# A two-layer graph kernel on one core: eight destination blocks gathered in place of nine, and 180 groups of edges counted in place of 177

## The chip, the core and the metric

The kernel runs on one core of one Trainium2 chip. Its engines are named as in the profile: PE multiplies matrices (PEld loads its stationary operand), DVE works on vectors, ACT applies functions and copies, POOL is the general engine, and SP issues DMAs. The metric is the device time of one execution in microseconds (us), as the median of several runs.

## The reference: what is computed

There are 6250 nodes with 128 features, 200000 edges with 128 features, and the edges are sorted by destination. The destinations are drawn as 6250 u² with u uniform, so low-numbered nodes receive many edges and high-numbered ones few.

```python
h = relu(layernorm(x))
x = x + relu(concat([h, segsum(h[src], dst), segsum(edge_attr, dst)]) @ W0.T + b0)
h = relu(layernorm(x))
h1 = relu(segmean(h[src], dst) @ W1_l + b1 + h @ W1_r)
h2 = relu(segmean(h1[src], dst) @ W2_l + b2 + h1 @ W2_r)
out = x + h2
```

So the sums over a node's in-edges are needed once for the edges' own features and three times (once in each of three layers) for the features of the source nodes.

## The kernel before

The nodes are cut into 49 blocks of 128 (`NB`), the edges into 196 groups of 1024 (`G`); a group holds eight tiles of 128 edges (`U`), so there are 1568 tiles.

**Two ways to sum over source nodes.** For 40 destination blocks (`NC`, the blocks 0 to 39) the kernel builds a dense matrix of counts: how many edges go from source node s to destination d. In every layer such a "dense" block then costs 49 products on PE, one for each source block, with the counts as the stationary operand and the split features (a high and a low half, 256 columns, 258 in the first layer) as the moving one: line 944. The last nine blocks (40 to 48), whose nodes have the fewest edges, are "listed" (`LISTS`): for each, a range of edge tiles is gathered by source index and summed with one product for each tile and block (line 1077).

**Stage 1, counting (up to line 816).** A set-up lays out the indices. Then a loop runs over the counted groups, 177 of them (`GC`). For each group DVE makes one-hot matrices of the sources (`sp`, line 520) and of the destinations (`sq`, line 520), weighs one of them (line 531), and, in groups where each tile has a window of its own (from group 84 on), makes a third small one-hot (`sc`). PE multiplies them tile by tile (line 755, and line 766 for the part that overlaps the tile before), and ACT copies the results into a ring buffer (line 781). The groups are cut into stretches, three groups each in the last regions; at the end of a stretch POOL writes the ring to `counts_d` in HBM (line 808). The last stretch is cut in two, the very last of one group. Between the counting products, and in proportion to the progress of the counting (`spent / shares`), PE sums the features of all 196 groups of edges (line 642; DVE makes the one-hot `hot` at line 633 and adds the result into `aggE` at line 648). The first-layer norm and product of a node block is done in every third group until all 49 are through.

**Stage 2, three layers of dense products (from line 819).** `neighbours(i)` runs over 3 x 40 dense blocks. The counts of a block come back from `counts_d` (1088 KB each, SP's queue, line 655), are widened from bytes to floats in six pieces (`widen`, line 876, some on DVE and some on ACT) and are multiplied (line 944). The rest of a block's layer, `after`, adds, norms and prepares the product of the next layer (transposition at line 460, weights at line 467); it is put between the products of the following blocks at fixed steps.

**The listed blocks** run beside the dense ones. Batches of up to three tiles (`batches`) are gathered by POOL with an indirect DMA for each tile (`gather`, line 1031), split in two halves and given a one-hot by ACT and DVE (`prepare`, lines 1048, 1049, 1055), and multiplied by PE (`sum_rows`, line 1077). The batches of a layer are spread evenly over the steps of that layer's dense products:

```python
begin = 4 * NB + NB // 2 if layer == 0 else 4 * NB
end = (NC - 2) * NB + 24 if layer < 2 else (NC - 1) * NB + 16
s = begin + (end - begin) * m // (len(batches) - 1)
```

**Which tiles a block needs, and which are counted, is fixed in constants.** The lists start at tile 1414, inside group 176, and every group up to 176 is counted, so that the two kinds of blocks meet. `GT` (176) is the group from which the indices of the listed tiles are loaded. On the chip the kernel tests that the constants fit the data (`lists_right`, line 535, and the tests from line 1131 on); where they don't, a general path computes everything again.

The constants `GC`, `GT`, `LISTS` stand at lines 36 to 40; `NC`, `NX`, `NE`, `NL` follow from them at lines 113 to 121, and the stretches at lines 123 to 138.

Of the kernel before, what the change touches and what calls it, by code (L numbers as in the profile page):

```python
# [32 lines left out]
NK = 2  # L33
NC3 = 3
PIECES = (("pair", 0, 4, 1), ("pair", 4, 8, 0), ("pair", 8, 12, 1), ("pair", 12, 17, 1), ("third", 0, 4, 0), ("third", 4, 8, 1))
GC = 177
GT = 176
LISTS = (
    (1414, 1433), (1432, 1451), (1449, 1468), (1466, 1484), (1483, 1501), (1499, 1518), (1517, 1535), (1533, 1550), (1549, 1563),
)  # L40
LATER = (1, 0, 0, 1, 0, 1)
FIRST = (1, 1, 1, 1, 0, 1)
# [45 lines left out]
def kernel(ctx: ExitStack, tc: tile.TileContext, x, srcl, dstl, edge, w0t, b0, w1l, b1, w1r, w2l, b2, w2r, out):  # L88
# [25 lines left out]
    NC = NB - NT  # L114
    NX = (G - GT) // 2
    assert 2 * NX == G - GT and U * NX <= P
    live_in_last = U - unused // P
    NE = sum(t1 - t0 for t0, t1 in LISTS)
    NL = (2 * NX - 1) * U + live_in_last
    assert LISTS[-1][1] == GT * U + NL and LISTS[0][0] >= GT * U  # L120
    CU = GC * U
    win_of = lambda g: REGIONS[min(g // RUN, NR - 1)][4]
    regions = []
    for i, reg in enumerate(REGIONS):
        if i * RUN < GC:
            regions.append((i * RUN, min((i + 1) * RUN, GC) if i + 1 < NR else GC) + reg)
    SWMAX = max(r[5] for r in regions)
# [5 lines left out]
    place_of = lambda g: sum(U // n for n in size_of[:g])  # L133
    places = place_of(GC)
    g, ng, *reg = stretches.pop()
# [4 lines left out]
    while tiles:  # L140
# [6 lines left out]
        marks = sorted((j, u) for u, (_, m) in enumerate(batch) for j in m)  # L147
        batches.append((batch[0][0] - GT * U, len(batch), marks))
    assert sum(len(marks) for _, _, marks in batches) == NE
# [56 lines left out]
    lists = build.enter_context(tc.tile_pool(name="lists", bufs=1))  # L206
    p_e = lists.tile([P, GC, U, 2], F16, name="p_e")
    q_e = lists.tile([P, GC, U, 2], F16, name="q_e")
    w_e = lists.tile([P, GC, U, 2], I16, name="w_e")
# [374 lines left out]
    def list_load(h, s):  # L584


        for k, a in enumerate((srcl, dstl)):
            at_s = bass.AP(
                tensor=a.tensor, offset=a.offset + P // U * s * GU + (GT + h * NX) * U, ap=[[U, NX], [GU, P // U], [1, U]]
            )  # L590
# [942 lines left out]
```

## Time and profile before

| | us |
|---|---|
| median of 7 runs | 1444.36 (1441.41 to 1450.07) |
| profiled execution | 1437.95 |
| its span, first to last instruction | 1436.4 |
| counting with the sums of edges | from 33.7 to about 583 |
| first layer of dense products | 584.0 to 886.5 |
| second | 886.5 to 1173.2 |
| third | 1173.2 to 1430.4 |

A row of the view by groups gives the line of the code, engine, operation, what it writes and reads, its count, its busy time and the mean of one; the idle time of the engine just before follows. The view of stretches (windows) gives each engine's busy time between two moments. PE's instructions are pipelined and overlap, so the distance between two starts says more than the duration of one. In fp32 one product is two entries on PE.

### The profile page before, as it was taken

The numbers are of one execution on the slowest core, as the hardware profiler recorded it, in microseconds if no ns is written. First come the engines' busy times: TensorE is split into PE (matmuls) and PEld (weight loads), VectorE is DVE, ScalarE is ACT, GpSimd is POOL, SyncE is SP. The second block draws the span as 40 slices with busy tenths as digits, with TensorE's granted clock in tenths as the row PEclk, the third lists the DMA queues.
The fourth block names the chain that finished last, engine by engine and source line by source line (L and its number), as shares of the span: only waits on it lengthen the run. The fifth ranks groups of instructions, "written<-read, shape, count | busy, mean of one in ns | idle before, by whom it ended". The sixth has DMA issues, their size and how long they took to land.

```text
span 1436.4 us, 37444 instructions
## 1 busy us (share of the span) xinstructions
PE 1395.3 (97%) x12457; PEld 1365.8 (95%) x12457; DVE 1152.3 (80%) x3006; ACT 933.1 (65%) x2253; POOL 693.1 (48%) x921
## 2 busy tenths in 40 slices
PE   7999999989999999899999999999999999999998
PEld 6899999889999999799999999999999999999998
DVE  8888899878898999878877787667876777777774
ACT  5434444557777777777777778666677686666663
POOL 4545676400000000366566640688887407777771
PEclk9999999999999999999999999999999999999999
DMA  2988899978999999877777766776777657777772
GB/s 77 291 269 291 283 316 323 306 268 310 329 314 311 346 348 372 294 259 246 238 245 243 245 219 213 259 258 216 231 237 235 221 193 260 267 250 261 251 253 72
DMA packets 173764, 374.02 MB, mean 260 GB/s; under 512 B 29451, under 2 KB 118985, under 8 KB 154234
## 3 DMA queue, kind: packets, MB, share of 16 engines
q1 hardware_dynamic: 121454, 268.72, 56.2%
q0 software_dynamic: 22336, 88.52, 18.1%
q10 hardware_dynamic: 29772, 14.31, 3.5%
q8 instruction: 100, 1.64, 0.5%
q14 instruction: 102, 0.84, 0.2%
HBM read 289.32 MB, written 82.13 MB: 259 GB/s over the span
## 4 chain that ended last, share of the span: by engine, by line
PE 68%; DMA 20%; issue 7%; ACT 2%; DVE 2%; POOL 0%; POOLq 0%; ACTq 0%; SPq 0%; DVEq 0%
PE ps L944 44%; DMA counts_d<-ring 17%; PE pe L642 11%; PE ps_t L1077 4%; PE pz L467 3%; PE pu L755 2%; PE pt L366 1%; DMA rows_t<-rows_d,row_i 1%; ACT wide L876 1%; DMA edge_t<-in_edge 1%; PE pu L467 1%; PE pz L460 1%; DVE wide L876 1%; PE ps L941 0%; DMA src_i<-in_src 0%
## 5 line engine op out<-in xcount | busy, mean ns | idle before, releaser
L944 PE MATMUL ps<-terms,wide 128*128 128x256 f32 (+1 forms) x5760 | 793.5, 290 | 3.4 <-DVE wide L876 1.7
L944 PEld LDWEIGHTS ps<-terms,wide 128*128 128x128 f32 x5760 | 740.0, 197 | 8.6 <-issue 1.9
L1031 POOL DMA_INDIRECT rows_t<-rows_d,row_i x447 | 505.6, 1131 | 297.4 <-issue 103.9
L642 PE MATMUL pe<-hot,edge_t 128*128 128x128 f32 x3136 | 472.9, 288 | 2.9 <-DMA edge_t<-in_edge 1.2
L642 PEld LDWEIGHTS pe<-hot,edge_t 128*128 128x128 f32 x3136 | 395.4, 192 | 6.4 <-issue 1.6
L876 ACT CAST wide<-c 128x1024 fp32r<-128x1024 uint8 x239 | 285.3, 1205 | 97.3 <-PE ps L944 87.0
L781 ACT CAST ring<-pu 128x170 f32 (+5 forms) x736 | 205.5, 282 | 86.8 <-PE pu L766 46.5
L876 DVE CAST wide<-c 128x1024 fp32r<-128x1024 uint8 x241 | 174.4, 726 | 73.6 <-PE ps L944 71.1
L755 PE MATMUL pu<-sq,sp 128*128 128x102 bf16 (+7 forms) x1416 | 170.5, 219 | 11.1 <-DVE r L470 3.8
L876 ACT CAST wide<-c_early 128x1024 fp32r<-128x1024 uint8 x118 | 140.6, 1204 | 52.4 <-PE ps L944 36.8
L808 POOL DMA_DIRECT2D counts_d<-ring x50 | 27.3, 545 | 293.7 <-ACT ring L781 213.1
L788 POOL TENSOR_TENSOR ring<-ring,fore 128x17 int32 x280 | 118.2, 422 | 82.0 <-ACT fore L776 39.2
L520 DVE TENSOR_TENSOR sq<-iota,q_e 128x816 bf16<-128x816 f16 (+7 forms) x177 | 123.5, 698 | 7.7 <-PE pu L766 7.2
L755 PEld LDWEIGHTS <-sp 128*128 128x128 bf16 x1416 | 118.9, 98 | 10.4 <-DVE sq L531 3.6
L520 DVE TENSOR_TENSOR sp<-iota,p_e 128x1024 bf16<-128x1024 f16 x177 | 121.7, 687 | 4.7 <-PE pu L755 2.2
L876 DVE CAST wide<-c_early 128x1024 fp32r<-128x1024 uint8 x122 | 88.2, 724 | 36.1 <-PE ps L944 35.1
L1055 DVE TENSOR_TENSOR tw<-rows_t,tw 128x384 fp32r<-128x384 f32 x153 | 83.2, 544 | 26.3 <-ACT tw L1048 24.8
L766 PE MATMUL pu<-sc,sp 128*128 128x17 bf16 x745 | 96.1, 172 | 0.0
L633 DVE TENSOR_TENSOR hot<-iota,rel 128x64 f32<-128x64 f16 (+13 forms) x196 | 94.5, 483 | 0.0
L790 ACT CAST ring<-pu 128x68 f32 (+5 forms) x280 | 63.3, 248 | 37.8 <-ACT fore L776 16.2
L1049 DVE TENSOR_TENSOR hot_t<-iota_p,slot_e 128x384 fp32r<-128x384 f16 (+1 forms) x153 | 87.4, 571 | 0.0
L1077 PE MATMUL ps_t<-tw,hot_t 128*128 128x256 f32 (+1 forms) x483 | 83.8, 283 | 0.0
(198 smaller groups left out, 1400.2 us busy)
## 6 DMA issues: line engine op xcount, KB each, us to landing
edge_t<-in_edge SPq DMA_DIRECT2D x196, 512.0 KB
c<-counts_d SPq DMA_DIRECT2D x80, 1088.0 KB
c_early<-counts_d SPq DMA_DIRECT2D x39, 1088.0 KB
rows_d<-feats ACTq DMA_DIRECT2D x147, 64.0 KB
r_d<-r SPq DMA_DIRECT2D x147, 64.0 KB
own<-r_d SPq DMA_DIRECT2D x147, 64.0 KB
counts_d<-ring POOLq DMA_DIRECT2D x5, 1462.0 KB
rows_t<-rows_d,row_i POOLq DMA_INDIRECT x447
```

Of the source, the lines that this page charges most:

```text
L520: made = nc.vector.tensor_tensor(to.rearrange("p t (c two) -> p t c two", two=2), iota[:, :m].rearrange("p (c two) -> p c two", two=2).uns ...
L633: nc.vector.tensor_tensor(hot[:, : U * win].rearrange("p (u w) -> p u w", w=win), iota[:, :win].unsqueeze(1).to_broadcast([P, U, win]), re ...
L642: mm = nc.tensor.matmul(ps[:, :P], e[:, u, :], hot[:, u * win : u * win + P], start=u == 0, stop=u == U - 1)
L755: mm = nc.tensor.matmul(pu[:, i * HALF : i * HALF + nq], sp[:, t, :], sq[:, t, :nq], start=t == t0, stop=t == t0 + n - 1 and n > 1,)
L766: mm = nc.tensor.matmul(pu[:, i * HALF : i * HALF + NJ], sp_b[:, t, :], sc[:, slot + 1 - len(last_tiles) + j0, :NJ], start=False, stop=j0 ...
L781: put = nc.scalar.copy(ring[:, bass.ds(to_put[(g - g0) * U + t0], nq)], pu[:, i * HALF : i * HALF + nq])
L788: add = nc.gpsimd.tensor_tensor(to, to, fore[:, i, :], op=ALU.add)
L876: copied = copy(t[:, : p1 - p0], two)
L944: dense = nc.tensor.matmul(ps[:, :m], counts, terms_of(s, s + 1)[:, 0, :m], start=s == 0, stop=s == NB - 1)
L1031: it = nc.gpsimd.indirect_dma_start(out=rows[:, u, :], out_offset=None, in_=rows_d[layer][:, :], in_offset=bass.IndirectOffsetOnAxis(ap=ro ...
L1049: made = nc.vector.tensor_tensor(hot[:, :k, :], iota_p.unsqueeze(1).to_broadcast([P, k, P]), slot_e[:, e : e + k].unsqueeze(2).to_broadcas ...
L1077: mm = nc.tensor.matmul(ps[:, :width], hot[:, k, :], tw[:, u, :width], start=begins, stop=ends)
```

## The change

`GC` goes from 177 to 180, `GT` from 176 to 178, and the first pair is taken out of `LISTS`:

```diff
-GC = 177
-GT = 176
+GC = 180
+GT = 178
 LISTS = (
-    (1414, 1433), (1432, 1451), (1449, 1468), (1466, 1484), (1483, 1501), (1499, 1518), (1517, 1535), (1533, 1550), (1549, 1563),
+    (1432, 1451), (1449, 1468), (1466, 1484), (1483, 1501), (1499, 1518), (1517, 1535), (1533, 1550), (1549, 1563),
 )
```

Block 40 becomes a dense block: `NC` is 41, and there are 123 turns of `neighbours` in place of 120. The listed tiles are 131 (1432 to 1562) in place of 149, their products 142 in place of 161 per layer, and their batches 45 in place of 51. The groups 177 to 179 are counted too; the stretches at the end are 168, 171, 174 (three groups each), 177 (two) and 179 (one), where they were 168, 171 (three each), 174 (two) and 176 (one), so one more ring is written. In the order of the source blocks, block 40 moves from the first to the last place of its piece of the widened counts.

## The prediction

> **What bounds the kernel now.** I read the busy time of each engine by stage first, then the chain of waits inside a quiet stage, then the order of time on PE and DVE in one group of the counting, and last what PE waits for. The stages (stretch, its length, then busy time and count of instructions for PE, PEld, DVE, ACT, POOL, the granted clock, DMA share, GB/s):
>
> ```profile
> 33.70:583.00 549.30, 528.47 (x5467) 510.86 (x5465) 484.04 (x1312) 327.71 (x1356) 162.01 (x353) 0.99 0.90 309
> 584.00:886.50 302.50, 297.81 (x2362) 293.33 (x2363) 237.51 (x713) 220.76 (x378) 165.04 (x152) 1.00 0.76 247
> 886.50:1173.20 286.70, 286.00 (x2272) 281.84 (x2271) 212.17 (x486) 203.82 (x329) 183.49 (x164) 1.00 0.71 232
> 1173.20:1430.40 257.20, 257.18 (x2128) 256.88 (x2126) 187.36 (x414) 161.35 (x174) 166.62 (x149) 1.00 0.71 232
> ...
> 504.30:550.50 46.20, 46.20 (x507) 45.51 (x506) 42.71 (x89) 35.80 (x119) 3.21 (x6) 1.00 0.98 354
> 550.50:577.40 26.90, 25.59 (x278) 24.73 (x277) 25.51 (x51) 18.81 (x61) 1.20 (x3) 1.00 0.92 351
> ```
>
> In the three layers (rows two to four) PE is full, at a granted clock of 1.00, while DVE has 21 to 27% and ACT 27 to 37% left. In the counting PE and DVE are both near their ends; in the last eight groups (the last row, 26.90 us, so 3.36 a group) they are equally full. "Busy" on PE can hide waits, so I take its cost from distances between starts. The chain in the third layer gives two clean ones:
>
> ```profile
> 1179.91 17.78 PE ps L944 x147
> 1197.69 0.36 PE ps_t L1077 x3
> ```
>
> 147 dense products follow each other in 17.78 us: 0.121 each. Three products of listed tiles take 0.36 with nothing lost on either side: 0.12 each.
>
> In the last region of the counting, PE in order of time:
>
> ```profile
> 564.32 0.92 PE L642 MATMUL pe<-hot,edge_t 128*128 128x128 f32 x6
> 565.07 0.24 PE L755 MATMUL pu<-sq,sp 128*128 128x187 bf16 x1
> 565.15 0.17 PE L766 MATMUL pu<-sc,sp 128*128 128x17 bf16 x1
> 565.18 0.24 PE L755 MATMUL pu<-sq,sp 128*128 128x187 bf16 x1
> 565.26 0.17 PE L766 MATMUL pu<-sc,sp 128*128 128x17 bf16 x1
> 565.28 0.69 PE L642 MATMUL pe<-hot,edge_t 128*128 128x128 f32 x4
> 565.81 0.24 PE L755 MATMUL pu<-sq,sp 128*128 128x187 bf16 x1
> ```
>
> A counted tile is a pair of products, and two pairs go from 565.07 to 565.28: 0.105 a tile. Six entries of edge sums take 0.75 (564.32 to 565.07), four take 0.53 (565.28 to 565.81): 0.11 an entry, and 0.09 more each time PE turns from counting to edges. DVE over the same group:
>
> ```profile
> 563.88 0.77 DVE L633 TENSOR_TENSOR hot<-iota,rel 128x592 f32<-128x592 f16 x1
> 564.56 0.69 DVE L520 TENSOR_TENSOR sp<-iota,p_e 128x1024 bf16<-128x1024 f16 x1
> 565.17 0.93 DVE L520 TENSOR_TENSOR sq<-iota,q_e 128x1504 bf16<-128x1504 f16 x1
> 566.02 0.23 DVE L648 TENSOR_TENSOR aggE<-aggE,pe 128x74 f32 x1
> 566.16 0.69 DVE L531 TENSOR_TENSOR sp<-sp,w_e 128x1024 bf16<-128x1024 bf16 x1
> 566.76 0.23 DVE L520 TENSOR_TENSOR sc<-iota,carry 128x144 bf16<-128x144 f16 x1
> 566.91 0.77 DVE L633 TENSOR_TENSOR hot<-iota,rel 128x592 f32<-128x592 f16 x1
> ```
>
> It never rests here. By starts, counting takes 0.61 (`sp`) + 0.85 (`sq`) + 0.60 (weighing) + 0.15 (`sc`) = 2.21, an edge group 0.68 + 0.14 = 0.82. Last, everything that PE waits for in the first layer, and POOL's gathers over the whole run:
>
> ```profile
> PE pz L460 <- ACT h L449: 2.2, 3, 1.8
> PE ps L944 <- DVE wide L876: 1.7, 4, 0.5
> PE ps L944 <- DVE aggE L648: 1.1, 1, 1.1
> PE ps L944 <- DVE terms L892: 0.5, 1, 0.5
> ...
> L1031 POOL DMA_INDIRECT rows_t<-rows_d,row_i x447 | 505.6, 1131 | 297.4 <-issue 103.9
> ```
>
> No wait of PE names a gathered row or its split (`tw`), here or in the other two layers (the second has three of 0.2, the third none).
>
> **The change, part by part.** *Block 40 dense (adds, on the path).* 49 products in each of three layers: 147 x 0.121 = 17.8 us. PE has no idle time to put them in. The block's norm, transposition and weights are done for a listed block too, and its product with `aggE` (line 941, before line 1081) as well: these only move, at nothing.
>
> *Its tiles are no longer listed (removes, on the path).* 161 - 142 = 19 products less per layer, 57 in all: 57 x 0.12 = 6.8 us back. The layers so gain 17.8 - 6.8 = 11.0.
>
> *Off the path in the layers.* Added: 18 widened pieces (nine on ACT at 1.20, nine on DVE at 0.73, the group rows' means), three `alone` copies at 0.27, and three loads of 1088 KB on SP's queue. Removed: 18 batches (ACT 0.52, DVE 0.55 + 0.55 each) and 54 gathers at 1.13 with 0.30 of issue on POOL. ACT: +10.8 - 9.4; DVE: +7.4 - 19.8; POOL: -77. The idle time of ACT and DVE (82 and 65 us in the first layer alone) hides what is added; without that cover ACT's balance would cost 1.4. The loads stand in SP's queue among those of own rows and x, four blocks ahead; at the third layer's 232 GB/s one takes 4.8 us, 14.4 in all if nothing covered them, but the DMA share is 0.71 and the gathers dropped are 54 x 64 KB, as many bytes. The batches sit at other steps of the layer (39 apart instead of 33), so the transpositions of listed blocks meet other products; of waits on ACT there are now 2.8 us in layers one and two, and I take their change as nothing, bounded by 3 either way.
>
> *Three more counted groups.* The sums of edges stay at 196 groups; they are only spread over 180. PE gets 24 tiles x 0.105 = 2.5 and about 12 more turns x 0.09 = 1.1: 3.6. DVE gets 3 x 2.21 = 6.6. ACT gets 24 copies of 0.32 (7.7), with 30% free. If PE sets the pace throughout, the stage grows by 3.6; if DVE does, by 6.6. If the new groups run at today's 3.36 and the thinner edge work gives the other 177 nothing, by 10.1. If the work falls into PE's idle time (20.3 us, the sum of PE's rows in the view of waits from 33.7 to 583, mostly for the first layer's `hT` and `r` and for one early `sq`), by nearly 0. A gain is excluded: PE, DVE and ACT all get more work here and none gets less. PE is full in the earlier regions and level with DVE in the last, so I take the middle of 3.6 and 6.6: **5.1**, with 0 and 10.1 as ends.
>
> *One more ring write.* 1598 KB on POOL's queue, 4.6 us at 354 GB/s. POOL mostly waits for ACT there (46 us of ACT against 16 of an earlier write from 504 to 583), so the write lies beside counting. The last two stretches keep their sizes (two groups and one), and what queues behind the last writes on POOL, the first gathers, is needed blocks later; the first block's counts are loaded 14 groups before the end, as now. Nothing.
>
> *Set-up.* The index tables are 180 columns wide, not 177: 12 copies on ACT at 0.8 and 192 products at 0.08 grow by 1.7%: 0.4, on the path. One index column less per load of lists: nothing.
>
> **Sum.** 11.0 + 5.1 + 0.4 = 16.5 on the profiled execution's 1437.95, so 1454.5. That execution lies 6.4 below the median of the runs shown; on 1444.36 the same sum gives **1460.9 us**, 1.1% slower.
>
> Two rules of the Trainium skill were weighed. In "TensorE: Matmul & The Clock Gate", Back-to-back issue gap, an isolated product of N columns takes N/2.4 + 2.5 ns, 109 ns for 256; the row has 121. As an estimate by that page the 147 and the 57 would be 16.0 - 6.2 = 9.8, and the whole 1459.7; the row decides. "DMA: Bandwidth & Descriptors", Rules for kernel authors, says that transfers under 64 KB mostly pay overhead and should be coalesced, which speaks for dropping 54 gathers of just that size; it would give POOL's 77 us to the kernel if they were on the path, and the waits of PE show that they are not.
>
> **The rivals.**
> - *The counting pays in full, or its end slips* (15%): the new groups run at 3.36 and nothing comes back, 10.1 + 11.0 + 0.4 = 21.5, 1465.9. For it: DMA share 0.98 at 504 to 550 and DVE without rest in the last groups, where all new work goes. Against: PE, not DVE, is full in the earlier regions, and 196 edge groups over 180 instead of 177 take 1.7% of its edge work out of each.
> - *The counting is almost free* (8%): 11.0 + 0.4, and the 2.8 us of waits for ACT go as well: 1453 to 1456. For it: 20.3 us of waits. Against: those end on the first layer's chain and stay.
> - *The other side: the gathers pace the layers* (4%). POOL works 167 us and issues 37 of the third layer's 257, after 46 us of waiting for rows: its queue is full. If a late row held PE, 18 gathers less a layer at 1.43 would bring 25.7 a layer, 77 in all, and the time 1384; it decides from 16.5 of 77 on. Against: a gather that is late shows as PE waiting at line 1077, and that wait is absent.
> - *The change doesn't do what it says* (1%): a test on the chip fails and everything is computed again. With the reference's destinations, tile 1432 begins at node 5243 (it must be 5184 to 5247) and tile 1440 at 5301 (at least 5248), and a whole last three-group stretch reaches 166 nodes of 177. The general path would take many times the kernel's time.
>
> **How the numbers follow.** The forecast has 72%. A kernel this size tells 0.3%, 4.3 us, from no change. All cases but the last two are slower by more; with waits I can't see, 92% slower, 3% within, 5% faster. The range goes from the nearly free counting, 1454.5, to the full price with 1.6 for the scatter of medians, 1467.5.
>
> **What would show it.** Line 944 at 6027 products and 0.121 from start to start; line 1077 at 426; the layers some 3.7 us longer each (306, 290.5, 261), the counting ending near 588 to 589. Wrong would be: the counting 10 or more longer; a PE wait at line 1077 that is gone; a new wait of line 944 on a load or on `wide`; or the first block's start later than the last edge sum by more than now (1.1).

## The result and the profile after

| | before | after |
|---|---|---|
| median, us | 1442.52 (46 runs, 1435.66 to 1450.07) | 1457.23 (18 runs, 1453.59 to 1462.48) |
| ratio after / before | | 1.0102, 95% interval 1.0089 to 1.0115 |
| profiled execution, us | 1437.95 | 1461.09 |

The change makes the kernel 14.7 us slower; forecast were 16.5, and 1460.9 for the time. The two profiled executions lie on opposite sides of their medians (4.6 below, 3.9 above), so they differ by 23.1, and 8.4 of that is scatter.

The profile after by stages: the stretch, its length, then busy time and count of instructions for PE, PEld, DVE, ACT, POOL, the granted clock, DMA share and GB/s. The first row is the counting, the others are the three layers.

```profile
35.00:596.00 561.00, 535.20 (x5518) 514.41 (x5515) 488.96 (x1321) 336.53 (x1380) 161.30 (x354) 0.99 0.89 306
597.17:903.30 306.13, 302.83 (x2391) 298.55 (x2392) 232.57 (x703) 221.34 (x375) 146.18 (x134) 0.99 0.75 244
903.30:1192.90 289.60, 289.22 (x2303) 285.46 (x2302) 210.24 (x479) 204.04 (x327) 156.13 (x146) 1.00 0.70 229
1192.90:1453.63 260.73, 260.73 (x2158) 260.36 (x2156) 182.92 (x406) 161.15 (x171) 148.57 (x131) 1.00 0.70 229
```

The layers grew from 302.5, 286.8 and 257.2 to 306.1, 289.6 and 260.7: by 3.6, 2.8 and 3.5, 9.9 in all. PE is full in them as before. In the chain of the third layer a product still has the same price. (Each product of line 944 is one entry: 6027 of them for 41 blocks of 49 in three layers. Two entries a product holds for the sums of edges, line 642, with 3136 entries for 1568 tiles.) 147 dense products and three listed ones read:

```profile
1199.65 17.75 PE ps L944 x147
1217.40 0.36 PE ps_t L1077 x3
```

All that PE waits for in the first layer after is 4.9 us, no item of which is a gathered row; in the second layer it is one wait of 0.3, in the third none:

```profile
PE ps L944 <- DVE wide L876: 2.1, 3, 1.1
PE ps L944 <- DVE aggE L648: 1.7, 1, 1.7
PE ps L944 <- DVE terms L892: 0.6, 1, 0.6
PE ps L944 <- ACT end_ring L781: 0.5, 1, 0.5
```

POOL's gathers fell by the 54 that were dropped, and POOL's waits grew in their place (the last part of the row):

```profile
L1031 POOL DMA_INDIRECT rows_t<-rows_d,row_i x393 | 441.0, 1122 | 367.0 <-DVE tw L1055 103.7
```

The first dense product stands at 597.2 in place of 584.0, and what PE waits for just ahead of it, the last sum of edges, grew from 1.09 to 1.73; first the kernel before, then the changed one:

```profile
584.01 0.37 PE L944 MATMUL ps<-terms,wide 128*128 128x258 f32 x1 [1.09 <-DVE aggE L648]
```

```profile
597.17 0.36 PE L944 MATMUL ps<-terms,wide 128*128 128x258 f32 x1 [1.73 <-DVE aggE L648]
```

Of the difference of the medians, 14.7, the layers take 9.9, and 4.8 is left for the counting and the set-up, if all of the scatter lies there.

**Where the counting's time went.** DVE starts one `sp` (line 520) for each group, so these starts are a clock of the counting. I read them from DVE's work in order of time; the last two columns are the kernels of the experiments e11 and e10 below, which differ only in `GC`, 177 and 180. Times in us.

| from the start of `sp` of group | before | after | e11 (177) | e10 (180) |
|---|---|---|---|---|
| 0 to 84 | 229.5 | 233.5 | 231.0 | 231.2 |
| 84 to 96 | 46.3 | 42.2 | 47.9 | 42.1 |
| 96 to 168 | 241.0 | 240.8 | 241.0 | 240.3 |
| 168 to 176 | 26.9 | 27.6 | 26.8 | 28.8 |
| 176 to 179, the three more | none | 10.6 | none | 9.8 |
| from the last `sp` to the first dense product | 6.6 | 7.5 | 7.2 | 9.1 |

So the three groups cost at least their full pace, about 3.5 each (9.8 to 14.0 over the six profiles with 180 groups whose work is whole). In groups 96 to 168 the thinner edge work gives nothing back that shows: 240.1 to 242.2 in these six, 240.8 to 242.6 in the four with 177 groups and nine lists. In the first 84 groups the four took 229.1 to 231.0 and the six 227.6 to 238.0; whether the more in most of them is scatter or a price is open. What comes back, comes between groups 84 and 96. There one group (92) took 8.3 before and takes 3.4 after. DVE's work in order of time (start, duration, engine, line, operation, and in brackets the idle time ahead of it and what ended it) shows why; first the kernel before:

```profile
291.40 0.50 DVE L633 TENSOR_TENSOR hot<-iota,rel 128x336 f32<-128x336 f16 x1
293.85 0.49 DVE L434 BATCH_NORM_STATS2 st<-x_c 128x6 f32<-128x128 f32 x2 [1.94 <-DMA x_c<-in_x]
294.25 0.16 DVE L436 BATCH_NORM_AGGREGATE mv<-st 128x2 f32<-128x6 f32 x1
294.33 0.26 DVE L434 BATCH_NORM_STATS2 st<-x_c 128x6 f32<-128x128 f32 x1
...
294.98 0.26 DVE L470 TENSOR_TENSOR r<-pu,b_sb 128x128 f32<-128x128 f32 x1
```

Four norms of the first layer (lines 434 and 436; some are behind the dots) stand together here in DVE's program, ahead of `r` (line 470) of an earlier block. The norms wait for a load of x; `r`, which would empty a PSUM buffer (`pu`) that PE needs for the next counted tiles, waits behind them. PE meanwhile stands, by its own work in order of time:

```profile
290.11 1.36 PE L642 MATMUL pe<-hot,edge_t 128*128 128x128 f32 x10
295.30 0.24 PE L755 MATMUL pu<-sq,sp 128*128 128x102 bf16 x1 [3.82 <-DVE r L470]
```

In the changed kernel DVE has `r` at its turn, and the norm that waits for the load of x comes later, with no `r` close behind it:

```profile
295.58 0.50 DVE L633 TENSOR_TENSOR hot<-iota,rel 128x336 f32<-128x336 f16 x1
296.00 0.16 DVE L446 RECIPROCAL rstd<-rstd 128x1 f32<-128x1 f32 x1
296.07 0.27 DVE L470 TENSOR_TENSOR r<-pu,b_sb 128x128 f32<-128x128 f32 x1
...
303.88 0.30 DVE L434 BATCH_NORM_STATS2 st<-x_c 128x6 f32<-128x128 f32 x1 [1.76 <-DMA x_c<-in_x]
```

The load is late in both (1.94 and 1.76); what differs is what stands behind it. Neither line was edited: with another number of groups the order of DVE's program is another one. The four norms ahead of an `r` around group 93 are found in the built order of the kernel before (with gathers or, as e6, e8 and e11, with plain loads) and of the kernels with ten and with seven lists (e2, e12), whose group 92 takes 8.2 to 10.1, and of e4, where it takes 6.9; and not in the kernels with 180 groups whose work is whole (after, e1, e5, e7, e9, e10), whose group 92 takes 3.4 to 3.7. (In e3 one norm waits 2.6 there, and group 92 takes 6.0.) No run moved these instructions alone; that their order is the cause rests on these traces.

### The profile page after: what moved, and what is told of

Read it like the earlier page. It is cut to its first block, busy times and chain, and to the rows that moved or that the text cites. A ratio compares the mean times of both kernels' runs of the same rounds, so it can differ in the third digit from the quotient of the medians.

```text
span 1459.5 us, 37634 instructions
## 1 busy us (share of the span) xinstructions
PE 1414.5 (97%) x12595; PEld 1381.6 (95%) x12595; DVE 1146.1 (79%) x2991; ACT 943.0 (65%) x2268; POOL 628.3 (43%) x868
## 5 line engine op out<-in xcount | busy, mean ns | idle before, releaser
L944 PEld LDWEIGHTS ps<-terms,wide 128*128 128x128 f32 x5904 | 755.1, 197 | 10.2 <-issue 2.6
L1031 POOL DMA_INDIRECT rows_t<-rows_d,row_i x393 | 441.0, 1122 | 367.0 <-DVE tw L1055 103.7
L876 ACT CAST wide<-c 128x1024 fp32r<-128x1024 uint8 x245 | 291.5, 1204 | 111.0 <-PE ps L944 99.4
L781 ACT CAST ring<-pu 128x170 f32 (+5 forms) x760 | 213.2, 283 | 85.3 <-PE pu L766 51.9
L876 DVE CAST wide<-c 128x1024 fp32r<-128x1024 uint8 x247 | 178.7, 726 | 91.2 <-PE ps L944 88.3
L755 PE MATMUL pu<-sq,sp 128*128 128x102 bf16 (+7 forms) x1440 | 174.5, 220 | 11.7 <-ACT ring L790 3.7
L755 PEld LDWEIGHTS <-sp 128*128 128x128 bf16 x1440 | 121.2, 99 | 14.7 <-issue 5.6
L1055 DVE TENSOR_TENSOR tw<-rows_t,tw 128x384 fp32r<-128x384 f32 x135 | 73.3, 543 | 28.0 <-ACT tw L1048 27.4
L790 ACT CAST ring<-pu 128x102 f32 (+5 forms) x280 | 62.8, 248 | 39.8 <-ACT fore L776 17.2
L531 DVE TENSOR_TENSOR sp<-sp,w_e 128x1024 bf16<-128x1024 bf16 x124 | 85.0, 685 | 0.1
L766 PEld LDWEIGHTS <-sp 128*128 128x128 bf16 x769 | 70.2, 97 | 7.6 <-issue 3.6
```

What stands on the lines that cost most here:

```text
L531: nc.vector.tensor_tensor(pairs, pairs, w_e[:, g].bitcast(BF16).unsqueeze(2).to_broadcast([P, U, m // 2, 2]), op=ALU.mult)
L755: mm = nc.tensor.matmul(pu[:, i * HALF : i * HALF + nq], sp[:, t, :], sq[:, t, :nq], start=t == t0, stop=t == t0 + n - 1 and n > 1,)
L766: mm = nc.tensor.matmul(pu[:, i * HALF : i * HALF + NJ], sp_b[:, t, :], sc[:, slot + 1 - len(last_tiles) + j0, :NJ], start=False, stop=j0 ...
L781: put = nc.scalar.copy(ring[:, bass.ds(to_put[(g - g0) * U + t0], nq)], pu[:, i * HALF : i * HALF + nq])
L876: copied = copy(t[:, : p1 - p0], two)
L944: dense = nc.tensor.matmul(ps[:, :m], counts, terms_of(s, s + 1)[:, 0, :m], start=s == 0, stop=s == NB - 1)
```

## The experiments

One fact is needed to read the numbers: in the sessions of the experiments the unchanged kernel before took 1518.4 to 1540.6 us, not 1442.5. Each experiment is therefore held against the kernel before timed on the same chip in the same session. What differs in those sessions is the subject of the second half; why it differs is not known.

**e1: 180 groups counted, all nine lists kept.** This is the counting half of the change alone.

```diff
-GC = 177
+GC = 180
```

> The kernel before with 180 groups counted and all nine blocks still listed, so the counting alone is changed. My theory (PE full in the early regions, DVE level with it in the last): 5.5 us slower than before, 1448, all of it before the first dense product; the three layers stay at 302.5, 286.7 and 257.2 within 1. Against the change itself, which differs only in block 40, it is 10 to 11 faster. If DVE alone paces the counting: 7 slower. If the new groups run at today's 3.36 and nothing comes back: 10.5 slower. If the 13 us by which the first dense product starts later in the profile of the changed kernel (597.2 against 584.0) are the price of the counting: 13 slower, and the layers can then not be worth 10 more.

Measured: 1544.92 (12 runs) against 1540.58, ratio 1.0031 (0.9994 to 1.0068): +4.3, interval about -0.9 to +10.5. It leans to the forecast, but can't exclude the full price.

**e2: ten lists.** The step in the other direction: block 39 is gathered too, with 176 groups counted. The last two lines only give a small tile of the tests on the chip a single buffer.

```diff
-GC = 177
-GT = 176
+GC = 176
+GT = 174
 LISTS = (
-    (1414, 1433), ...
+    (1397, 1415), (1414, 1433), ...
-            void = small.tile([P, U], F32, name="void")
+            void = small.tile([P, U], F32, name="void", bufs=1)
```

> The step the other way: block 39 is listed too (tiles 1397 to 1414, 166 listed tiles), 39 dense blocks, 176 groups counted. If PE's products alone decide, each layer is 5.9 - 18 x 0.12 = 3.7 us shorter (299, 283, 253.5) and the counting 1 to 2 shorter: 12 to 13 faster, 1430. The rival that POOL's queue of gathers paces a layer once it is full: 17 more gathers of 1.43 in a third layer where POOL has 203 of 257 us taken and begins some 35 us late; then PE waits at line 1077 there, the third layer is 10 to 25 longer than 253.5, and the whole is between 1430 and 1455. I hold the second the likelier.

Measured: 1589.18 (4 runs), ratio 1.03 (1.0232 to 1.0368), 48.6 slower where the sum of prices makes the layers about 11 shorter; both alternatives of the expectation missed. The layers take 340.8, 334.0 and 317.9. (The first dense product also stands late, at 599.4, with one group fewer counted; why isn't known.) In the third layer:

```profile
1274.30:1592.20 317.90, 285.77 (x2097) 274.70 (x2095) 189.45 (x422) 159.90 (x177) 185.35 (x166) 0.93 0.56 188
```

PE is busy 286 of 318 and its clock is granted at 0.93. But for 0.2, a wait for split rows (`tw`), all that it waits for there is put down to "issue" and carries no name of a row:

```profile
PE ps L944 <- issue: 28.2, 51, 1.9
PE ps_t L1077 <- issue: 2.7, 4, 1.0
PE ps_t L1077 <- DVE tw L1055: 0.2, 1, 0.2
```

**e3: the change without the weighing on DVE (line 531).**

```diff
-            if nq < P and n > 1:
-                weigh(sq[:, :, :even], g, even)
-            else:
-                weigh(sp, g, P)
```

> The changed kernel without the weighing on DVE in all 180 groups (the counts of three source blocks then fall into one byte, so the sums are not those of the reference). DVE loses 180 instructions, 0.43 to 0.69 us each, about 95 us; PE loses nothing. If DVE paces the counting throughout, the stage shrinks by 80 to 95; if PE does, by 0 to 5; if both are level, as I hold, by 10 to 25, down towards PE's own work of about 525 us in a stage of 561.

Measured: 1496.34 (4 runs), ratio 0.9694 (0.963 to 0.9759); the change itself has 0.9737 (0.9694 to 0.978, e5, in another session). The first dense product stands at 597.3, as in the profile after. DVE's busy time in the counting fell to 396 and the stage did not shorten:

```profile
36.00:595.00 559.00, 535.68 (x5497) 517.27 (x5497) 396.14 (x1130) 333.82 (x1378) 132.95 (x354) 0.99 0.88 306
```

**e4: the change with seven of eight edge tiles summed**, so 392 entries less on PE.

```diff
+            if u == U - 1:
+                continue
-            mm = nc.tensor.matmul(ps[:, :P], e[:, u, :], hot[:, u * win : u * win + P], start=u == 0, stop=u == U - 1)
+            mm = nc.tensor.matmul(ps[:, :P], e[:, u, :], hot[:, u * win : u * win + P], start=u == 0, stop=u == U - 2)
```

> The changed kernel with seven in place of eight products in each group's sum of edges (an eighth of the edges' features is left out). PE loses 196 x 2 entries of 0.112 = 44 us; DVE loses nothing. If PE paces the counting throughout: 40 to 44 faster; if DVE does: 0 to 8; if both are level: 20 to 35.

Measured: 1502.25 (4 runs), ratio 0.9732 (0.9662 to 0.9802), no faster than the change. The first dense product stands at 608.2:

```profile
36.00:605.00 569.00, 503.14 (x5085) 473.99 (x5086) 482.78 (x1312) 334.43 (x1378) 167.80 (x354) 0.97 0.87 301
```

Both expectations missed. Taking work from DVE alone or from PE alone buys nothing that shows. The starts of `sp` say where it went: without the weighing, groups 96 to 168 take 237.9 in place of 240.8, a gain of 2.9, and 3.5 are lost again between the last `sp` and the first dense product (11.0 against 7.5). With fewer edge products the same groups take 250.5, nearly 9 of it between groups 144 and 150, where PE waits 5.3 for a weighed `sp` and DVE 7.1 for ACT ahead of an `r`. The granted clock, too, was lower in e4's counting, 0.97 in place of 0.99. Both kernels also have a new order of instructions, so they are not clean removals. Removing both kinds of work at once wasn't tried; what paces the counting stays open.

**e5: the changed kernel beside the kernel before**, as it stands.

> The changed kernel again, beside the kernel before on one chip. On the chip of the first four runs the kernel before took 1540, its layers with nine lists 320, 322 and 296 (first look above), while two kernels with eight lists had layers of 312 to 313, 303 to 304 and 276 to 279, 45 us less in all. If that chip's extra time goes with the number of gathers, the change is faster there: 1540 + 4 - 45 = 1500, ratio 0.974. On a chip where the kernel before takes about 1442 and its layers 302.5, 287 and 257, the change is 15 slower, ratio 1.010, by my sum of 16.5: counting 5.5 and layers 11. If the extra time of that chip has nothing to do with the lists (a slower clock or memory), the ratio is 1.010 on both.

Measured: 1500.19 (6 runs) against 1539.16, ratio 0.9737 (0.9694 to 0.978). Here the same change is 39.0 us *faster*. Its layers take 313.8, 302.3 and 273.5, 33.1 more than in the profile after:

```profile
599.60:913.40 313.80, 304.65 (x2391) 297.80 (x2392) 233.12 (x703) 220.33 (x375) 142.28 (x133) 1.00 0.74 239
913.40:1215.70 302.30, 292.91 (x2302) 287.63 (x2301) 209.75 (x479) 203.65 (x326) 153.79 (x146) 0.99 0.68 219
1215.70:1489.20 273.50, 267.26 (x2158) 264.88 (x2156) 182.15 (x406) 161.11 (x171) 153.10 (x131) 0.98 0.67 218
```

**e7: 180 groups, nine lists, again** (the edit of e1).

> 180 groups counted, nine lists, beside the change on one chip. It was 4.3 us slower than before (ratio 1.0031, interval 0.9994 to 1.0068) on the slow chip. My theory: 5.5 slower, the counting stage longer and the layers as before. DVE alone pacing: 7 slower; nothing coming back: 10.5 slower. The change against this one gives the price of block 40 alone: 10 to 11 slower where the layers are 302.5, 287 and 257, some 45 faster where they are 320, 322 and 296.

Measured: 1547.12 (12 runs) against 1539.16, ratio 1.0039 (1.0009 to 1.0069): +6.0 by the ratio, 1.4 to 10.6 (8.0 by the medians). So counting three groups more costs a little, and the dropped list brings more than the whole 39 us: 46.9, from e7 to e5. With nine lists the layers are longest:

```profile
594.90:924.20 329.30, 306.89 (x2362) 298.36 (x2363) 237.58 (x712) 220.12 (x378) 166.04 (x151) 0.98 0.71 228
924.20:1250.10 325.90, 296.50 (x2272) 288.40 (x2272) 212.05 (x486) 203.09 (x329) 174.19 (x164) 0.96 0.63 204
1250.10:1544.60 294.50, 273.55 (x2127) 267.30 (x2126) 185.70 (x414) 160.48 (x174) 168.41 (x149) 0.97 0.62 202
```

They have the instructions of before's layers (302.5, 286.8, 257.2) and take 103 us more.

**e6: plain loads in place of gathers.** A batch of listed tiles is loaded from consecutive rows, by one DMA on SP's queue. The bytes are the same, but they are other rows, so the listed sums are not the reference's. POOL's indirect DMAs are gone, and with them a rule that put the tests on the chip behind the gathers on POOL (e8 keeps it).

```diff
-        tc.add_manual_dep(it.ins, latest["POOL"].ins.name, IN_ORDER, reason="the first layer goes before the tests")
...
-        for u in range(n):
-            it = nc.gpsimd.indirect_dma_start(
-                out=rows[:, u, :],
-                out_offset=None,
-                in_=rows_d[layer][:, :],
-                in_offset=bass.IndirectOffsetOnAxis(ap=row_i[:, t + u : t + u + 1], axis=0),
-            )
...
+        b = m % (NB - BT)
+        it = nc.sync.dma_start(
+            rows[:, :n, :], rows_d[layer][b * P : (b + n) * P, :].rearrange("(u p) f -> p u f", p=P)
+        )
```

> The kernel before with nine lists, but each batch of up to three tiles is loaded with one plain DMA of consecutive rows on SP's queue in place of three indirect DMAs on POOL (so the listed sums are of other rows than the reference's). Bytes, splits, one-hots and products stay. If the gathers on POOL are what lengthens the layers on the slow chip, its layers fall from 320, 322 and 296 to about 302, 287 and 257, 90 us less; if the chip is slow by itself, they stay within 5. On a chip with layers of 302.5, 287 and 257 nothing changes by more than 3, as PE never waits for a gathered row there.

Measured: 1442.88 (4 runs) against 1539.16, ratio 0.9353 (0.9302 to 0.9405): 96.3 us go, and the layers are 304.7, 286.3 and 257.2, those of the kernel before in the result's measurement. So what the sessions differ in goes when the gathers go.

**e8: the same plain loads on POOL's queue, one for each tile.** It has as many DMAs as before, from the same engine.

```diff
-            it = nc.gpsimd.indirect_dma_start(
-                out=rows[:, u, :], ...
-            )
+            b = (t + u) % (NB - 1)
+            it = nc.gpsimd.dma_start(rows[:, u, :], rows_d[layer][b * P : (b + 1) * P, :])
```

> The kernel before with nine lists, each tile loaded with one plain DMA of 128 consecutive rows issued by POOL in place of the indirect one (the listed sums are of other rows). It tells apart two readings of the plain loads on SP, which gave 1443 beside 1539: if any DMA whose descriptors POOL makes slows the other engines, the layers stay near 320, 322 and 296 and the time near 1540; if it is the indirect ones alone, the layers fall to 303 to 305, 286 to 287 and 257 and the time to 1440 to 1450.

Measured: 1440.22 (4 runs) against 1518.44, ratio 0.9489 (0.9436 to 0.9542). The number of DMAs, their bytes and POOL's queue are thus not to blame; that they are indirect is. The row of these loads (x447) and the third layer beside them, from two views:

```profile
L1032 POOL DMA_DIRECT2D rows_t<-rows_d x447 | 271.5, 613 | 525.2 <-DVE tw L1051 360.4
```

```profile
1171.70:1428.90 257.20, 257.14 (x2128) 256.84 (x2126) 185.85 (x415) 161.27 (x174) 82.09 (x137) 1.00 0.70 229
```

An indirect DMA differs in POOL's time (1.1 against 0.61 us) and in its rows, which lie scattered. The two were not separated.

**e9, e10, e11: the change, its counting half and the kernel before, all with e6's plain loads.** Without indirect DMAs the sum of the prediction can be tested without the price that varies by session. e11 is e6 again, e10 adds `GC = 180`, e9 adds the whole change.

```diff
 # e10, to e6's edit
-GC = 177
+GC = 180
```

```diff
 # e9, to e6's edit
-GC = 177
-GT = 176
+GC = 180
+GT = 178
-    (1414, 1433), (1432, 1451), ...
+    (1432, 1451), ...
```

> The change (eight lists, 180 groups) with the plain loads on SP, against nine lists and 177 groups with the same loads, where PE is not slowed by gathers. My sum: 16.5 slower, 11.0 in the layers (3.7 each) and 5.5 before the first dense product. If the counting gives nothing back: 21.5. If the plain loads leave something of the gathers' price, the layers grow by less than 3 each.

> Nine lists and 180 counted groups, with the plain loads on SP: the price of the counting alone, free of gathers. My sum: 5.5 slower than nine lists and 177 groups with the same loads, layers the same within 1. DVE alone pacing: 7; nothing coming back: 10.5; PE alone pacing: 4.

> Nine lists and 177 groups with the plain loads on SP, as measured at 1442.9 on four runs: the base of the other two on this chip. All theories: 1440 to 1446, layers near 304, 286.5 and 257.

Measured: e11 1442.35, e10 1448.76, e9 1460.30 (6 runs each in one session on one chip: 1439.4 to 1446.8, 1445.3 to 1454.6, 1453.5 to 1466.9; the ratios to before are 0.9502, 0.9546 and 0.9606, each to about 0.0043 or 6.6 us either way). Counting costs 6.4, where 5.5 were forecast with the set-up (six runs that spread over 7 and 9 us don't tell this from the rivals' 4 or 10); the block made dense 11.5, where 11.0 were; the whole 17.95, where 16.5 were. The layers of e9:

```profile
603.30:908.00 304.70, 301.15 (x2391) 296.97 (x2392) 231.09 (x703) 221.33 (x375) 7.96 (x17) 1.00 0.78 251
908.00:1197.60 289.60, 289.20 (x2302) 285.42 (x2301) 207.96 (x479) 203.87 (x326) 0.50 (x1) 1.00 0.70 225
1197.60:1458.30 260.70, 260.70 (x2158) 260.43 (x2157) 181.10 (x406) 161.22 (x171) 0.00 (x0) 1.00 0.70 225
```

and those of e11:

```profile
587.90:888.20 300.30, 297.73 (x2361) 293.31 (x2362) 235.39 (x712) 220.74 (x378) 8.31 (x17) 1.00 0.80 254
888.20:1174.60 286.40, 285.84 (x2272) 281.83 (x2271) 211.28 (x486) 203.43 (x329) 1.17 (x1) 1.00 0.71 229
1174.60:1431.80 257.20, 257.20 (x2128) 256.92 (x2127) 185.56 (x415) 161.30 (x174) 0.00 (x0) 1.00 0.71 229
```

They differ by 4.4, 3.2 and 3.5, 11.1 in all. The first of these is the least certain: e6, the same program as e11, had 304.7 there, e10 300.3. In the second and third layers these lengths equal those with gathers in the result's measurement (289.6 and 260.7, 286.8 and 257.2) within 0.4: there the gathers were hidden.

**e12: seven lists,** the next step the same way. (One more edit, not shown, copies a value in the tests on the chip where the range of a reduction would be empty.)

```diff
-GC = 177
-GT = 176
+GC = 182
+GT = 180
-    (1414, 1433), (1432, 1451), (1449, 1468), ...
+    (1449, 1468), ...
```

> One step further: block 41 dense too, seven lists from tile 1449 (114 tiles), 182 groups counted, indirect gathers as in the change. Over the layers with plain loads (about 844 for nine lists, 855 for eight), the layers of the kernels with indirect gathers were longer by 160 (ten lists), 94 and 105 (nine) and 35 (eight) on these chips. If that falls on by some 60 a list, nothing is left at seven, and the time is that of the products: the change with plain loads, 1460, + 11 for the block + 4 for two groups = 1475, with 5 to 10 for what may be left: 1475 to 1485, faster than both kernels there (ratio to before about 0.965 where before takes 1520 to 1540). If the price halves only, 1490 to 1495; if it stays at 35, 1510, slower than the change. On a chip where the kernel before takes 1442, it would be 30 slower than before.

Measured: 1501.14 (12 runs) against 1518.63, ratio 0.9895 (0.9864 to 0.9925). That is the time of eight lists in e5 (1500.19), and the expected 1475 to 1495 missed. The kernel before, though, took 20.5 less in e12's session than in e5's: against it seven lists are 17.5 faster, where eight were 39.0. The two were not run in one session. Taking the price of a dense block from e9 to e11, its layers without indirect DMAs would be about 866 as an estimate; they took 887.6. No version was best in every session: nine lists are faster than eight where gathers are hidden, and slower than eight or seven where they aren't.

**What the indirect DMAs do in these sessions.** POOL and PE side by side in the third layer of e1, in order of time. POOL issues gathers one after the other, with its usual pause of 0.30:

```profile
1255.63 0.95 POOL L1031 DMA_INDIRECT rows_t<-rows_d,row_i  x1 [0.30 <-issue]
1256.89 0.95 POOL L1031 DMA_INDIRECT rows_t<-rows_d,row_i  x1 [0.30 <-issue]
1258.15 0.95 POOL L1031 DMA_INDIRECT rows_t<-rows_d,row_i  x1 [0.30 <-issue]
```

PE does one to three dense products in between and then stands, about once for each gather, for nothing that the profile names:

```profile
1255.39 0.52 PE L944 MATMUL ps<-terms,wide 128*128 128x256 f32 x3 [0.87 <-issue]
1256.83 0.28 PE L944 MATMUL ps<-terms,wide 128*128 128x256 f32 x1 [0.92 <-issue]
1258.25 0.37 PE L944 MATMUL ps<-terms,wide 128*128 128x256 f32 x1 [1.13 <-issue]
```

In the profile after, POOL issues with the same durations and pauses while PE runs its 147 products from 1199.65 on without a break:

```profile
1206.67 0.96 POOL L1031 DMA_INDIRECT rows_t<-rows_d,row_i  x1 [0.30 <-issue]
1207.93 1.12 POOL L1031 DMA_INDIRECT rows_t<-rows_d,row_i  x1 [0.30 <-issue]
1209.35 0.96 POOL L1031 DMA_INDIRECT rows_t<-rows_d,row_i  x1 [0.30 <-issue]
```

So POOL's side shows nothing: a gather takes 1122 ns in the mean after, 1131 before, 1119 in e7. The price appears on the other engines. Their instructions hardly get longer (piece by piece, `wide` takes 723 ns on DVE and 1207 on ACT in e7, 726 and 1205 before; a dense product of the third layer 291 in e7 and 284 in e11): they start later. The lists and their price, as the layers' excess over the same layers with plain loads:

| lists | gathers | layers, us | with plain loads | excess |
|---|---|---|---|---|
| 10 (e2) | 498 | 992.7 | 833 (estimate: e11's less e9's step of 11.1) | 160 |
| 9 (e1, e7) | 447 | 937.7, 949.7 | 843.9 (e11) | 94, 106 |
| 8 (e5) | 393 | 889.6 | 855.0 (e9) | 35 |
| 7 (e12) | 342 | 887.6 | 866 (estimate: e9's and a step of 11.1) | 22 |

It falls much faster than the count of gathers, also between rows of one session (e2 and e1, e7 and e5); the last row is from a session in which the kernel before took 20 less. By medians, nine lists cost 96.3 (e6 against the kernel before), eight 39.9 (e5 against e9), so the change brings 56.4 and costs 17.95: 38.5, next to the 39.0 measured. This sorts the same medians into two terms; it proves nothing more, as e6 and e11, which alone could differ in it, are one kernel.

## Why the prediction was right, and where it wasn't

- **The whole.** 14.7 measured for 16.5; 1457.2 for 1460.9, within the range. This holds for sessions in which gathers are hidden. Two of the signs that were to show the prediction wrong stand in the profile after all the same: the counting is 11.7 longer (561.0 for 549.3), its end near 596 and not 588 to 589, and the first product waits 1.73 for the last sum of edges, not 1.1. As much as 8.4 of it may be the scatter of the two executions.
- **Block 40 dense, its tiles no longer listed: 17.8 - 6.8 = 11.0.** Right in mechanism and size: 9.9 between the two profiles, 11.1 by layers between e9 and e11 (6.8 against e6's profile), 11.5 by medians. From start to start, the 147 more dense products took 16.7 and the 57 listed ones gave back 6.3.
- **Work on ACT, DVE and the loads hidden; moved batches nothing, within 3.** Right: PE's waits in the layers after are 4.9, 0.3 and 0.
- **Three more counted groups: 5.1, the middle of PE's 3.6 and DVE's 6.6.** The size fits by the medians (4.8 with the set-up in the result; 4.3, 6.0 and 6.4 in e1, e7 and e10), though none of e1, e7 and e10 alone excludes 4 or 10, and the profiles put it higher: the first dense product stands at 584.0 to 588.8 in the four with 177 groups and nine lists and at 590.8 to 603.3 in the six with 180, 10.5 apart in the mean. The reason is not right. The three groups cost 9.8 and 10.6, the price of the rival "the counting pays in full", and the thinner edge work gave nothing that shows. About 4 to 6 came back between groups 84 and 96. Three statements failed. That PE or DVE sets the pace was not borne out (e3 and e4 take 93 us from DVE and 32 from PE and gain nothing that shows, though in a new order). "A gain is excluded" overlooked what a new order can bring. And the 20.3 us of waits did not "end on the first layer's chain and stay": the wait for `r` at 295 was one of them, and it went, while others came, 24.2 in all in the profile after. The sum that the traces show has terms of opposite sign, and the value between my bounds was reached by luck.
- **Set-up 0.4.** Not to be seen: the first `sp` starts at 34.0 in both e10 and e11, and the first 84 groups vary by 10 between profiles with the same 180 groups.
- **Gathers hidden; the other side at 4%.** Right where the result was measured: 54 gathers less gave nothing. Wrong in the experiments' sessions, and by its sign: there the change is 39.0 faster. The step that failed is the argument that "a gather that is late shows as PE waiting at line 1077". The gathers were not late; the engines beside them were held up, which is a price that no wait for a row shows. The rival named the right operation, and the wrong sign by which to know it.
- **The two rules.** For "TensorE: Matmul & The Clock Gate" the row's 0.121 held (0.121 after). The estimate by the page's 109 ns, 9.8 for the layers, is not told from 11.0 by the 9.9 to 11.5 measured. The advice on small transfers in "DMA: Bandwidth & Descriptors" was worth nothing in the result; in e6 the coalesced loads were 96.3 faster, but e8, with the small ones kept, was as fast: it was not the size.

## What to carry to other kernels

A change in a loop's length can change the order of instructions at places that the edit never touched (here DVE's), so a stall that stands in a profile can leave, or arrive; count such stalls as their own term, and ask what is queued behind each late load. Price an added iteration at the end of a stage at its full pace, as here, unless a run shows that the work taken from the others returns.

A resource that looks hidden because no wait names it is only hidden in the sessions seen. Where two versions trade one resource for another, replace the suspected operation by a plain one of the same bytes, and price the rest without it.

## What the runs showed of the hardware

- With indirect DMAs on POOL, instructions of PE, DVE and ACT started late in some sessions and not in others: with 447 of them the same layers took 846.5 us in the result's measurement, and 937.7 and 949.7 in e1 and e7. Plain DMAs of the same size, number and queue cost nothing (844.1 in e8). PE's waits are put down to "issue", those of ACT and DVE in part to "remote" (in e7 32 us ahead of `wide` on DVE and 14 on ACT, none in the kernel before); the granted clock was 0.96 to 0.98 in e7's layers, 0.93 in e2's last. Whether the scattered rows or the way POOL issues them is the cause, and what differs between sessions, is open. The Trainium skill, in "SBUF — State Buffer", section "SBUF: two separate sides", has DMA and compute on separate ports that cannot contend, and explains an apparent slowdown of a DMA by a DVE operation that keeps POOL from writing descriptors. Here POOL's instructions did not get longer, and PE and ACT waited, which neither covers; that SBUF is the place isn't shown.
- The excess is far from proportional: 160, about 100 and 35 us for 498, 447 and 393 gathers, and 22 for 342 in a session where the kernel before lost less.
- The chips or sessions differ for one kernel: the kernel before had 1442.5 in the result's measurement, 1540.6, 1539.2, 1518.4 and 1518.6 in the four sessions of the experiments, two of these on the same chip (1539.2 and 1518.6). The kernels without indirect DMAs had 1442.9 and 1442.4 on two chips.
